# Cross-attention and feed-forward block: opening query sums reordered, gate weights loaded by SyncE

## The chip, the cores and the metric

One core of a Trainium2 chip runs the whole program. The metric is the time of one execution in device microseconds (us); lower is better. Engines are named as in the profile: PE (TensorE matmul) with PEld (its weight loads), DVE (VectorE), ACT (ScalarE), POOL (GpSimd) and SP (SyncE, which here only issues DMAs).

## The reference

The block is one transformer layer on x of 8 sequences, 128 tokens, 512 features, all in float32:

```
x = x + attn(layernorm(x), ctx) @ Wo          # 32 query heads, 8 key heads, head size 128
x = x + ffn(layernorm(x))
attn: q, k with rotary tables; logits = 30 * tanh(q.k * 0.0884 / 30); mask; softmax; times v
ffn:  (silu(x @ dq(w1).T) * (x @ dq(w2).T)) @ dq(w3).T        # 1376 hidden units
dq:   blocks of 64 weights; each weight, over its block's largest magnitude,
      is moved to the nearest of 16 levels and scaled back
```

So there are three parts of work: projections and attention, the rounding of w1, w2 and w3 to 16 levels, and the feed-forward products with the rounded weights.

## The kernel before, in words

**Number format.** Products run as three float32r matmuls (function product, L165): each operand is split into a high part (ScalarE cast, L155) and a low part (subtraction, L156, on VectorE or GpSimd, whichever the caller names). A product over 512 features is 12 matmuls of 128x128 by 512 columns.

**Stages.** First come the key and value projections of all heads and the four query products of the first unit (u = 0), with results in DRAM. Then the attention loop runs over N = 64 steps i (L763). A unit u is a key head kv and half of the batch; a step is one batch entry of one unit, with its four query heads (G = 4). A step issues, for TensorE and in this order: a query product of the next unit (q_proj, tile pq), the output projection of step i-3 (project, tile po), the transposition of step i-2 (turn, tile pt_a), the weighted values of step i-1 (values, tile pv) and the scores of step i (scores, tile pl). All engines run their instructions in program order, so what stands ahead of an instruction on its engine holds it back.

**What follows a query product.** rope (L455) copies the two halves of pq crosswise on ScalarE (L463, L464), multiplies by the cosine on VectorE (L465) and by the sine on GpSimd (L466), and returns the sum (L467), which the caller places. For the first two units the sum is on VectorE, and for u = 1 the cosine product stays in pq's own PSUM bank, so the bank is free only after the sum. pq and pt_a share two banks (tag q); pl, pt_y and others share one (tag s).

**What follows the scores.** Two ScalarE activations (tanh and exp, L682, L683) and the mask on GpSimd (L685); then the values matmuls, a reciprocal and a product on VectorE (tile ad, L694, L695), and the transposition.

**Opening steps.** Step 0 makes query products 0 and 1 of unit 1, step 1 product 2, step 2 product 3, step 3 none. The output projection weights of the first head (load_o, tile wo, named o 0 0 to o 0 3 in the table due) are split in these steps: the first two on VectorE, the last two on GpSimd. Step 0 splits the first at its end. In step 1 the third product's rope comes at the head, its sum behind the values, then the second weight's split. In step 2 the fourth product's rope comes behind the transposition and its sum behind the values.

**Quantization.** A generator (quantize, L376) rounds w1, w2 and w3 unit by unit. Each unit (up to 128x1024 values, tile w) is loaded by SyncE with its scales (tiles s_w), multiplied by the inverse scale on GpSimd (L206), compared with 15 bounds, one ScalarE activation (nm, L196) and one VectorE operation (nc, L202) each, multiplied by the scale on VectorE (L238 or L280) and split (a cast and a GpSimd subtraction, tile w3t or dqt). pump(n) runs the generator for n credits of about one bound each; it is called twice a step. The rounded w1 and w2 go to DRAM (w12t_d) and come back in the feed-forward part; the rounded w3 stays in SBUF. In a unit of w3 the next unit's weights and inverse scales are loaded at bound 6 (L234, L228), the product of L206 is at bound 13, and its own scales are loaded at bound 2.

**Feed-forward.** xn (L150) are the normalized rows, transposed into pt_y and split into xT (normal2, turned). gate_up (L731) makes a gate product (tile pg) and an up product (tile pu) of one of two batch halves and one of 11 blocks of 128 hidden units. load_w12(h) (L726) loads the two 512 KB weights of block h, in a pool of six buffers shared with the query weights. Blocks 0 to 2 are loaded in the last three attention steps, the others in the loop of L868 at n = 1, 2, 5, 7, 9, 11, 13 and 15, after that iteration's pump. The loads are issued by GpSimd. At last the down products (tile pd, L893, L903) use w3t.

Of the kernel before, what the change touches and what calls it, by code (L numbers as in the profile page):

```python
# [11 lines left out]
F32 = mybir.dt.float32  # L12
# [11 lines left out]
G = NH // NKV  # L24
# [38 lines left out]
def block_kernel(ctx: ExitStack, tc: tile.TileContext, x, ctxt, mask, wq, wk, wv, wo, w1, w2, w3, w12t, w3_t,  # L63
                 rope_tab, nf_bias, out):
    nc = tc.nc
# [14 lines left out]
    w12t_d = dram.tile([NHT, 2, P, 2, KT, P], F32, name="w12t_d")  # L80
# [130 lines left out]
    class Down(Unit):  # L211
# [30 lines left out]
        def store(self, h):  # L242
            pool, tag, bufs = (f1, "w3t", 8) if h < 8 else (nf, "nf_t", 2) if h < 10 else (xp, "wide", 2)
            t = w3t[h] = pool.tile([P, 2, KT, P], F32R, tag=tag, name=f"w3t_{h}", bufs=bufs)
            own = t.rearrange("p i k c -> p i (k c)")[:self.p].rearrange("p i (c e) -> p i e c", e=4)
            split(own[:, 0], own[:, 1], self.part(self.w, h).rearrange("p (e c) -> p e c", e=4), Q)
# [44 lines left out]
    class Scales:  # L291
# [23 lines left out]
        def turn(self, tag):  # L315
            pt = bank(tag, f"pt_ar_{self.h}")[:2 * 16, :P]
            E.transpose(pt, self.s.rearrange("p t b -> p (t b)"), ident)

            def later():
                t = nf.tile([2 * 16, P], F32, tag="nf_st", name=f"art_{self.h}", bufs=1)  # L320
                S.copy(t, pt)
                nc.sync.dma_start(scale_d.rearrange("t j b h -> (t j b) h")[:, self.h * P:(self.h + 1) * P], t)
            stored.append(later)

    class Scales3:
# [3 lines left out]
        s = cp.tile([P, 2, nb], F32, name="ar3")  # L329
# [75 lines left out]
    def pump(n):  # L405

        credit[0] += n
        while credit[0] > 0:
            credit[0] -= next(stream, n + credit[0])
# [7 lines left out]
    def end_store():  # L417
        if stored:
            stored.pop()()
# [7 lines left out]
    with ExitStack() as c1:  # L427
# [41 lines left out]
        wqt, todo = {}, {}  # L469

        def load_q(kv, g):
            wqt[kv, g], todo["q", kv, g] = columns(wq, kv * G + g, f"wq_{kv}_{g}")

        def q_proj(u, g):
            kv, half = divmod(u, 2)
            if g == 0:
                qr[u] = a1.tile([P, 4, G, T], F32, tag="qr", name=f"qr_{u}", bufs=2)
            pq = bank("q", f"pq_{u}_{g}")
            w, t = wqt[kv, g], xT[half]
            product(pq, [((w[:, 0, k], w[:, 1, k]), (t[:, 0, k], t[:, 1, k])) for k in range(KT)])  # L480
            return lambda: rope(qr[u][:, :, g, :], pq, cosq, sgnq, f"q{u}_{g}", V if u < 2 else None, u == 1)


        with ExitStack() as c3:
# [134 lines left out]
            xn, turned = {}, {}  # L619
# [38 lines left out]
        def load_o(kv, g):  # L658
            h = kv * G + g
            raw = stage(wo[h * HD:(h + 1) * HD], [P, D], f"wo_{kv}_{g}")  # L660
            t = wot[kv, g] = at.tile([P, 2, D], F32R, tag="wo", name=f"wo_{kv}_{g}", bufs=8)
            todo["o", kv, g] = lambda: split(t[:, 0], t[:, 1], raw, Q if kv or g > 1 else V)

        def load_kv(kv):
            for half in range(2):
                krt[kv, half] = at.tile([P, 512], F32, tag="kr", name=f"krt_{kv}_{half}", bufs=4)
                nc.sync.dma_start(krt[kv, half], kr_d[kv, half])
            vt[kv] = at.tile([P, B, HD + 1], F32, tag="v", name=f"vt_{kv}")
            nc.sync.dma_start(vt[kv][:, :, :HD], v_d[kv])
            Q.memset(vt[kv][:, :, HD:], 1.0)  # L670

        def where(i):
            u, bb = divmod(i, 4)
            return u, u // 2, (u % 2) * 4 + bb, bb
# [12 lines left out]
        def values(i):  # L687
            u, kv, b, bb = where(i)
            ad[i] = at.tile([P, G, HD], F32, tag="ad", name=f"ad_{i}")
            pv = ps.tile([P, G, 256], F32, tag="pv", name=f"pv_{i}", bufs=1)  # L690
            for g in range(G):
                E.matmul(pv[:, g, :HD + 1], em[i][:, g], vt[kv][:, b], start=True, stop=True)  # L692
            rs = tp.tile([P, G], F32, tag="rs", name=f"rs_{i}")
            V.reciprocal(rs.unsqueeze(2), pv[:, :, HD:HD + 1])  # L694
            V.tensor_tensor(ad[i], pv[:, :, :HD], rs.unsqueeze(2).to_broadcast([P, G, HD]), ALU.mult)  # L695
# [5 lines left out]
        def project(i):  # L701
            u, kv, b, bb = where(i)
            po = bank("wo", f"po_{i}")
            product(po, [((aT[i][:, 0, g], aT[i][:, 1, g]), (wot[kv, g][:, 0], wot[kv, g][:, 1]))
                         for g in range(G)])
            V.tensor_tensor(acc[b], acc[b], po, ALU.add)
# [9 lines left out]
        def normal2(b, xn, tag):  # L716
            if b % 4 == 0:
                xT2[b // 4] = wide(f"xT2_{b // 4}")
            t = xT2[b // 4]
            own = slice(b % 4 * T, b % 4 * T + T)  # L720
            return transposed(t[:, 0, :, own], t[:, 1, :, own], xn, f"y{b}", tag)


        w12, hT, ups = {}, {}, []

        def load_w12(h):  # L726
            w12[h] = [wp.tile([P, 2, KT, P], F32R, tag="wq", name=f"w12_{h}_{j}", bufs=6) for j in range(2)]
            for j in range(2):
                nc.gpsimd.dma_start(w12[h][j], w12t_d[h, j])

        def gate_up(half, h, pool=None, between=None):  # L731
            t = xT2[half]
# [20 lines left out]
                V.tensor_tensor(hT[half, h // 4][:, h % 4], sg, pu, ALU.mult)  # L753
            return later

        due = {0: [("o", 0, 0)], 1: [("o", 0, g) for g in range(1, G)]}
        xn = {}

        def turned(ks, tags):
            for f in [normal2(k, xn[k], tag) for k, tag in zip(ks, tags)]:  # L760
                f()

        for i in range(N):  # L763
            u, kv, b, bb = where(i)
            s8 = i % 8
            if kv + 1 < NKV:
                if s8 == 0:
                    load_kv(kv + 1)
                if s8 < 4:
                    load_q(kv + 1, s8)  # L770
                else:
                    load_o(kv + 1, s8 - 4)
                due.setdefault(i + (2 if i < 4 else 1), []).append(("q" if s8 < 4 else "o", kv + 1, s8 % 4))
            tiles = {0: (0, 1), 1: (2,), 2: (3,), 3: ()}.get(i, (bb,)) if u + 1 < 2 * NKV else ()
            later = [q_proj(u + 1, g) for g in tiles]
            if i != 2:
                later = [f() for f in later[:1]] + later[1:]
            if i == 0:
                later.pop(0)()
            if i > 3:  # L780
                store()
                end_store()
            pump(1.5 if 2 < i < 58 else 1 if i == 58 else 0)
            if 0 <= i - 3:
                project(i - 3)
            if i in (59, 61):
                ln = LayerNorm((i - 59, i - 58), f"y{i - 59}")
            if 0 <= i - 2:
                turn(i - 2)
            if i == 2:  # L790
                later = [later[0]()]
            if 59 <= i < 63:
                ln.sums(i - 59)
            if 0 <= i - 1:
                values(i - 1)
            if i in (1, 2):

                later.pop(0)()
                if i == 1:
                    todo[due[1].pop(0)]()  # L800
            scores(i)
            if i == 0:
                later = [later[0]()]
            if i == 61:
                xn.update({k: pair.rows(k, "xn") for k in (0, 1)})
            for f in later:
                f()
            pump(1.65 if 2 < i < 58 else 2 if i == 58 else 0)
            if i == 62:
                turned((0, 1), "qq")  # L810
            if i in (60, 62):
                ln.finish(Q)
                pair = ln
            for k in due.pop(i, ()):
                todo[k]()
            if i >= 61:
                load_w12(i - 61)
# [3 lines left out]
        turned((2,), "s")  # L821
        turn(N - 2)
        values(N - 1)
        turned((3,), "s")
        ln = LayerNorm((4, 5), "y1")
        ln.sums(4)
        ln.sums(5)
# [40 lines left out]
    for n, (half, h) in enumerate(order):  # L868
        evac()
        evac = gate_up(half, h, f1)  # L870
        pump((3.6 if n < last - 3 else 2.6) if n > 0 else 0)
        store()
        if n in w12_at:
            load_w12(w12_at[n])
        if n >= last - 3:
            split_h(*to_split.pop(0))
# [4 lines left out]
    for b, i in down:  # L881
# [5 lines left out]
        for h in range(4 * i, min(NHT, 4 * i + 4)):  # L887
            m = min(P, H - h * P)
            t, s = w3t[h].rearrange("p i k c -> p i (k c)"), hs[b, i]
# [7 lines left out]
        elif i == 2:  # L897
            o = f1.tile([P, D], F32, tag="o", name=f"o_{b}", bufs=4)
# [41 lines left out]
```

## Time and profile before

| | |
|---|---|
| median of 3 runs | 783.3 us (782.45 to 1315.04) |
| profiled execution | 782.62 us, span 780.9 us, granted TensorE clock 1.000 |
| outside the span | 1.7 us |
| gate loads (w, L729) | 22 of 512 KB, 4.7 us median from issue to landing |
| s_w loads of 64 KB | 86, on SyncE |
| all DMA | 102.44 MB, mean 131 GB/s |

A timeline line of the profile has the start (us from the span's start), the duration, engine, line and operation, the tiles written and read, the shape and the number of instructions merged; in brackets stands the idle time ahead of it and what ended that. A line "A <- B: x, n, y" in a list of waits says that A waited for B x us in total, n times, y at most. Matmuls are pipelined, so consecutive ones overlap in the timeline; starts are the better measure.

### The profile page before, as it was taken

The page shows a single profiled execution, that of the slowest core. Times are in us where ns is not written, and L with a number is a line of the kernel's source. Part 1 is how long each engine was busy: PE and PEld are TensorE (multiplying, and loading weights), DVE is VectorE, ACT ScalarE, POOL GpSimd, SP SyncE. Part 2 cuts the span into 40 slices and gives each one's busy share as a digit, 9 for nine tenths or more (in the row PEclk, how much of TensorE's full clock was granted, in tenths as well). Part 3 has the DMA queues.
Part 4 walks back from the last instruction along what each step waited for, and adds up shares of the span by engine and source line. Part 5 has one row for each costly group of instructions (what it writes and reads, how often), then busy time and mean ns, then how long its engine had stood idle before and what let it go on. Part 6 is the DMA issues. An engine that isn't in the chain of part 4 may idle for free.

```text
span 780.9 us, 11199 instructions
## 1 busy us (share of the span) xinstructions
PE 775.2 (99%) x3737; PEld 627.7 (80%) x3737; DVE 626.8 (80%) x839; ACT 585.4 (75%) x821; POOL 468.3 (60%) x412
## 2 busy tenths in 40 slices
PE   9999999999999999999999999999999999999998
PEld 7888877878878787887888888878778888888887
DVE  6768877888887887888888878888778697899971
ACT  7458668888897979798787879898742686789740
POOL 3569537887878778877778787878651222332100
PEclk9999999999999999999999999999999999999999
DMA  7966753546255615536245523413123235633011
GB/s 231 300 206 199 220 160 99 174 124 176 56 173 138 199 45 165 148 93 208 65 146 159 155 71 112 134 60 116 60 103 108 61 97 166 179 118 112 1 54 55
DMA packets 73329, 102.44 MB, mean 131 GB/s; under 512 B 7832, under 2 KB 42840, under 8 KB 73272
## 3 DMA queue, kind: packets, MB, share of 16 engines
q1 hardware_dynamic: 70104, 90.19, 38.6%
q0 software_dynamic: 3168, 11.54, 4.7%
q8 instruction: 30, 0.49, 0.3%
q14 instruction: 27, 0.22, 0.1%
HBM read 79.32 MB, written 22.38 MB: 130 GB/s over the span
## 4 chain that ended last, share of the span: by engine, by line
PE 97%; DVE 1%; POOL 1%; ACT 1%; issue 0%; POOLq 0%
PE pq L172 22%; PE po L172 22%; PE pd L172 8%; PE pg L172 8%; PE pu L172 8%; PE pv L692 7%; PE pl L679 7%; PE pk L172 6%; PE pvp L172 6%; PE pt_a L162 3%; PE warm L91 0%; PE pt_x L162 0%; DVE xn_y L150 0%; PE pt_y L162 0%; DVE xT L156 0%
## 5 line engine op out<-in xcount | busy, mean ns | idle before, releaser
L202 DVE SCALAR_TENSOR_TENSOR nc_w<-nm_w,nc_w 128x1024 f32<-128x1024 bf16 (+1 forms) x238 | 284.6, 1196 | 56.5 <-ACT nm_w L196 45.4
L196 ACT ACTIVATE nm_w<-w_w,bias 128x1024 bf16<-128x1024 f32 (+1 forms) x255 | 275.8, 1115 | 25.8 <-POOL w_w L206 17.1
L172 PE MATMUL pq<-xT,wq 128*128 128x512 f32 x768 | 209.1, 422 | 0.0
L172 PEld LDWEIGHTS pq<-xT,wq 128*128 128x128 f32 x768 | 143.9, 188 | 55.8 <-issue 24.4
L172 PE MATMUL po<-wo,aT 128*128 128x512 f32 x768 | 188.7, 394 | 0.0
L172 PEld LDWEIGHTS po<-wo,aT 128*128 128x128 f32 x768 | 143.3, 188 | 33.3 <-issue 2.4
L685 POOL TENSOR_TENSOR th<-th,mt 128x512 f32<-128x512 f32 x64 | 83.6, 1307 | 86.0 <-ACT th L683 78.1
L466 POOL TENSOR_TENSOR rs_q<-rs_q,sgnq 128x512 f32<-128x512 f32 x64 | 82.5, 1289 | 15.1 <-ACT rs_q L464 15.1
L682 ACT ACTIVATE th<-pl 128x512 f32<-128x512 f32 x64 | 38.3, 598 | 51.0 <-PE pl L679 47.9
L467 POOL TENSOR_TENSOR qr<-rc_q,rs_q 128x512 f32<-128x512 f32 x56 | 72.6, 1297 | 0.0
L692 PE MATMUL pv<-vt,th 128*128 128x129 f32 x512 | 67.9, 276 | 0.1
L679 PE MATMUL pl<-qr,krt 128*128 128x512 f32 x128 | 65.6, 594 | 0.0
L172 PE MATMUL pg<-xT,w 128*128 128x512 f32 x264 | 63.8, 390 | 0.0
L172 PE MATMUL pu<-xT,w 128*128 128x512 f32 x264 | 63.5, 389 | 0.0
L692 PEld LDWEIGHTS pv<-vt,th 128*128 128x128 f32 x512 | 62.2, 192 | 0.7 <-POOL th L685 0.7
L172 PE MATMUL pd<-w3t,hs 128*128 128x512 f32 (+3 forms) x297 | 60.6, 366 | 0.0
L206 POOL TENSOR_TENSOR w_w<-w_w,s_w 128x1024 f32<-128x1024 f32 (+1 forms) x17 | 40.0, 2351 | 32.8 <-DMA s_w<-scale_d 31.2
L172 PEld LDWEIGHTS pd<-w3t,hs 128*128 128x128 f32 (+1 forms) x297 | 51.4, 189 | 9.2
L172 PEld LDWEIGHTS pu<-xT,w 128*128 128x128 f32 x264 | 49.5, 188 | 10.3
L172 PEld LDWEIGHTS pg<-xT,w 128*128 128x128 f32 x264 | 49.3, 188 | 10.1
L156 POOL TENSOR_TENSOR w3t<-w_w,w3t 128x512 fp32r<-128x512 f32 (+1 forms) x11 | 17.2, 1565 | 64.8 <-ACT w3t L155 64.8
L155 ACT CAST aT<-pt_a 128x512 fp32r<-128x512 f32 x64 | 36.5, 571 | 26.0 <-PE pt_a L162 26.0
(119 smaller groups left out, 1105.2 us busy)
## 6 DMA issues: line engine op xcount, KB each, us to landing
w12t_d<-dqt SPq DMA_DIRECT2D x22, 512.0 KB
w<-w12t_d POOLq DMA_DIRECT2D x22, 512.0 KB, 4.7
s_w<-scale_d SPq DMA_DIRECT2D x40, 256.0 KB
raw_wq<-in_L_xattn_Wq SPq DMA_DIRECT2D x32, 256.0 KB
raw_wo<-in_L_xattn_Wo SPq DMA_DIRECT2D x32, 256.0 KB
s_w<-scale_d SPq DMA_DIRECT2D x86, 64.0 KB
ws<-in_L_ffn_w SPq DMA_DIRECT2D x20, 256.0 KB
w_w<-in_w12t SPq DMA_DIRECT2D x10, 512.0 KB
```

The lines of the kernel that those rows point to most:

```text
L155: S.copy(hi, src)
L162: E.transpose(pt[:, k * P:(k + 1) * P], src[:, k * P:(k + 1) * P], ident)
L172: E.matmul(out, a, b, start=start and i + j == 0, stop=stop and i == n - 1 and j == 2)
L196: S.activation(m, self.w, AF.Relu, bias=bias[:self.p, i:i + 1], scale=BIG if up else -BIG)
L202: V.scalar_tensor_tensor(self.c, m, step, self.c, ALU.min, ALU.subtract if i == POS[0] else ALU.add)
L206: Q.tensor_tensor(self.w, self.w, self.s, ALU.mult)
L466: Q.tensor_tensor(s, s, every(sgn), ALU.mult)
L467: return lambda: (engine or Q).tensor_tensor(dst, c, s, ALU.add)
L679: E.matmul(pl, krt[kv, u % 2][:, bb * T:(bb + 1) * T], qr[u][:, bb].rearrange("p g t -> p (g t)"), start=True, stop=True)
L682: S.activation(th, pl, AF.Tanh, scale=ATTN_MULT / CAP)
L685: Q.tensor_tensor(em[i], em[i], mt.unsqueeze(1).to_broadcast([P, G, T]), ALU.mult)
L692: E.matmul(pv[:, g, :HD + 1], em[i][:, g], vt[kv][:, b], start=True, stop=True)
```

## The change

Four edits. The gate loads are issued by SyncE, with the tile viewed as float32. The first projection weight's split moves from the end of step 0 to step 1, directly behind the third query product's rope. The third query sum moves ahead of the values of step 1. The fourth query product's rope and sum move behind the scores of step 2. With these, the two pumps of step 3 run 0.5 and 2.65 credits in place of 1.5 and 1.65, and the last tile turned ahead of the feed-forward part takes a bank of tag q in place of s. The arithmetic is the same.

```diff
         def load_w12(h):
             w12[h] = [wp.tile([P, 2, KT, P], F32R, tag="wq", name=f"w12_{h}_{j}", bufs=6) for j in range(2)]
             for j in range(2):
-                nc.gpsimd.dma_start(w12[h][j], w12t_d[h, j])
+                nc.sync.dma_start(w12[h][j].bitcast(F32), w12t_d[h, j])
...
-        due = {0: [("o", 0, 0)], 1: [("o", 0, g) for g in range(1, G)]}
+        due = {1: [("o", 0, g) for g in range(G)]}
...
             if i == 0:
                 later.pop(0)()
+            if i == 1:
+                todo[due[1].pop(0)]()
             if i > 3:
                 store()
                 end_store()
-            pump(1.5 if 2 < i < 58 else 1 if i == 58 else 0)
+            pump(1.5 if 3 < i < 58 else 1 if i == 58 else 0.5 if i == 3 else 0)
...
-            if i == 2:
-                later = [later[0]()]
             if 59 <= i < 63:
                 ln.sums(i - 59)
+            if i == 1:
+
+                later.pop(0)()
             if 0 <= i - 1:
                 values(i - 1)
-            if i in (1, 2):
-
-                later.pop(0)()
-                if i == 1:
-                    todo[due[1].pop(0)]()
+            if i == 1:
+                todo[due[1].pop(0)]()
             scores(i)
-            if i == 0:
+            if i in (0, 2):
                 later = [later[0]()]
...
-            pump(1.65 if 2 < i < 58 else 2 if i == 58 else 0)
+            pump(1.65 if 3 < i < 58 else 2 if i == 58 else 2.65 if i == 3 else 0)
...
-        turned((3,), "s")
+        turned((3,), "q")
```

## The prediction

> **What bounds the kernel now.** I read the page first, then TensorE's own waits, then the stretches the change edits, engine by engine.
>
> ```profile
> PE 775.2 (99%) x3737; PEld 627.7 (80%) x3737; DVE 626.8 (80%) x839; ACT 585.4 (75%) x821; POOL 468.3 (60%) x412
> PE 97%; DVE 1%; POOL 1%; ACT 1%; issue 0%; POOLq 0%
> ```
>
> TensorE is 99% busy and is 97% of the chain that ended last. Only a hole in its stream, or a new one, can change the time. Its waits over the span, without the warm-up:
>
> ```profile
> PE pt_a L162 <- DVE qr L467: 0.6, 1, 0.6
> PE pt_y L162 <- DVE xT L156: 0.3, 1, 0.3
> ```
>
> Both lie where the change is. But busy time hides part of a hole, since a matmul lasts longer than its turn (0.39 us against 2.76 us for twelve, 0.23 each). So I compare starts, in the timeline of TensorE at the opening of attention, with those of a later step.
>
> ```profile
> 115.75 3.06 PE L172 MATMUL pq<-xT,wq 128*128 128x512 f32 x12
> ...
> 119.77 1.02 PE L679 MATMUL pl<-qr,krt 128*128 128x512 f32 x2
> 120.83 2.98 PE L172 MATMUL pq<-xT,wq 128*128 128x512 f32 x12
> 124.46 0.63 PE L162 MATMUL pt_a<-ident,ad 128*128 128x128 f32 x4 [0.65 <-DVE qr L467]
> ```
>
> Scores to transposition takes 119.77 to 124.46, 4.69 us. The same sequence later (131.21 less 0.46, to 134.37) takes 3.62. So 1.07 us is lost here: 0.2 net ahead of the product at 120.83, which waits for the bank of the second query sum, and 0.87 behind it, for the third. VectorE's timeline says why:
>
> ```profile
> 119.99 0.69 DVE L467 TENSOR_TENSOR qr<-pq,rs_q 128x512 f32<-128x512 f32 x1 [0.70 <-POOL rs_q L466]
> 120.60 1.70 DVE L156 TENSOR_TENSOR wo<-raw_wo,wo 128x512 fp32r<-128x512 f32 x1
> 122.22 0.69 DVE L465 TENSOR_TENSOR pq<-pq,cosq 128x512 f32<-128x512 f32 x1
> ...
> 123.03 0.69 DVE L695 TENSOR_TENSOR ad<-pv,rs 128x512 f32<-128x512 f32 x1
> 123.63 0.68 DVE L467 TENSOR_TENSOR qr<-pq,rs_q 128x512 f32<-128x512 f32 x1
> ```
>
> The first projection weight's split (1.70 us) sits ahead of the third query's product. The end of attention, GpSimd's timeline:
>
> ```profile
> 584.93 1.30 POOL L729 DMA_DIRECT2D w<-w12t_d  x2
> 586.24 1.30 POOL L685 TENSOR_TENSOR th<-th,mt 128x512 f32<-128x512 f32 x1
> ```
>
> The gate loads hold the last mask back 1.0 us (its exp ended at 585.23). TensorE there:
>
> ```profile
> 587.59 1.16 PE L692 MATMUL pv<-vt,th 128*128 128x129 f32 x8
> 589.08 0.66 PE L162 MATMUL pt_y<-ident,xn_y 128*128 128x128 f32 x4 [0.33 <-DVE xT L156]
> ```
>
> In the feed-forward part TensorE has no hole at all. The queue that gets the loads, SyncE's timeline:
>
> ```profile
> 692.86 0.83 SPq L234 DMA_DIRECT2D w_w<-in_w3t  x2
> 693.73 11.64 SPq L228 DMA_DIRECT2D s_w<-scale_d  x16
> ```
>
> GpSimd, and the product that uses gate load 9:
>
> ```profile
> 688.23 1.10 POOL L729 DMA_DIRECT2D w<-w12t_d  x2
> 691.28 1.56 POOL L156 TENSOR_TENSOR w3t<-w_w,w3t 128x512 fp32r<-128x512 f32 x1 [1.95 <-ACT w3t L155]
> 699.30 2.40 POOL L206 TENSOR_TENSOR w_w<-w_w,s_w 128x1024 f32<-128x1024 f32 x1 [6.46 <-DMA s_w<-scale_d]
> ```
>
> ```profile
> 695.30 2.88 PE L172 MATMUL pg<-xT,w 128*128 128x512 f32 x12
> ```
>
> SyncE's w_w load at 692.86 starts when GpSimd's split ends (691.28 + 1.56 = 692.84). Load 9 was issued at 688.23 on the other queue and did not care.
>
> **The change, part by part.** All sums are against the profiled execution: 782.62 us, span 780.9, 1.7 outside it. It is 0.7 below the 783.3 median of the runs shown.
>
> 1. Opening of attention, third query sum. VectorE has the same five pieces after 120.68, in another order: product (0.69), wo split, sum (0.68), reciprocal (0.17), ad (0.69). With no split ahead of it, the third product runs at 120.68 to 121.3. ScalarE's copies for it (0.58 each) move ahead of the wo cast and end at about 120.0, so GpSimd's rs product (1.28) ends at 121.4 and GpSimd then idles until mask 1 (about 122.6). The split costs 1.70 beside GpSimd work (row above), 1.14 in the next wo split at 124.23, and 0.68 is the same instruction with a PSUM source. Beside an idle GpSimd I take 0.8, nearest to 0.68, so sum 122.1, ad 122.9 to 123.7, transposition at about 123.9: gain 0.55. At 1.70 it starts at 124.75, loss 0.3; the cap is 0.8, where TensorE itself gets there.
>
> 2. Fourth query sum behind scores. The transposition of step 3 does not want its bank: a new tile takes the buffer that was handed back first in program order. (The scale loads at 622.60 wait for GpSimd's w_w product, L206, and start ahead of the VectorE product of the unit before, L238, at 625.75; rotation in turn would have waited for that.) Bank of transposition 0 is back in step 2 ahead of the fourth sum, so transposition 1 takes it, and the query product of step 4 takes the other. From scores 2 at T, by rows: tanh T+1.1 to 1.7, exp to 2.33, two copies to 3.55; GpSimd's mask to 3.7, rs product to 5.0, sum to 5.7. The step-4 product started at T+5.39 (125.82 to 131.21); it comes 0.5 late, of which 0.25 is absorbed by the issue gap that stands there anyway. The wq split of key head 1 also queues behind it on GpSimd (1.29 more, T+6.3), and the third matmul, at T+6.0, needs it. Cost 0.4; bounds 0 (the backlog is worked off) and 1.0 (the whole tile waited for). Mask 2 comes first, no loss. The pump of step 3 gives 0.5 and 2.65 in place of 1.5 and 1.65, the same 3.15: ScalarE has one 1.1 us instruction more behind exp 3; tanh 4 slips by at most that, with 3 us to its mask's reader. Nothing.
>
> Opening: -0.55 + 0.4 = -0.15; bounds -0.8 and +1.3.
>
> 3. End of attention. Three pairs of issues (1.29, 1.30, 1.13) leave GpSimd. Mask 63 runs at 585.27 to 586.57, its values at the natural 587.33 (0.43 behind the transposition at 586.90), 0.26 earlier. xn 2 and 3 took 2.80 beside the issues and 1.97 at 574.22 beside a mask alone, so VectorE is some 0.65 earlier too. The last turned tile goes to bank q, no longer waiting for the s tile's split: 587.33 + 0.90 = 588.23 in place of 589.08. The projection behind follows at 588.66, its third matmul wants aT 62's split at 589.1 (done 0.6 earlier than 589.63: just in time). Gain 0.8; bounds 0 (VectorE no earlier and the projection stalls instead) and 1.0.
>
> 4. Gate loads on SyncE. Loads 0 to 4 are early or wait for the same products as before. The scale loads behind load 4 are needed 20 us later (649.89). From load 5 on the place in SyncE's program counts, by the pump's credits: load 5 behind the w_w and s_w loads at 641.40, load 7 behind those at 665.79, load 9 behind those at 692.86; 6, 8 and 10 follow at once. How long a 512 KB load on SyncE takes to land is not shown. Below: 2.3 (last s_w issue 697.0 to GpSimd's start at 699.30, 64 KB). Above: 4.7 (the same load from GpSimd). I take the middle, 3.5.
>  - Load 5: issue 646.75, lands 650.25, wanted 651.78. Nothing, at 4.7 either.
>  - What loads 5 and 7 no longer do is share the DMA engines with the s_w loads ahead. In before, s_w's last issue at 646.3 was followed by GpSimd at 650.38, 4.1 later, against the 2.3 of the quiet case. So w_w's product comes 1.8 earlier, and VectorE, busy from 654.00 to 677.2 without a hole, with it; at the next unit the loads land 4 us earlier, and VectorE begins it about 3.3 earlier than 678.87.
>  - Load 7: w_w loads 1.75 earlier, issue 669.3, lands 672.8, wanted 673.54. Nothing; 1.1 to 2.3 without the catch-up.
>  - Load 9: GpSimd's split ends 692.84 - 3.3 = 689.5, two w_w and eight s_w issues take 4.55 (692.86 to 697.4), issue 694.1, lands 697.6; wanted 695.30. A new hole of 2.3. Bounds: split at 688.5 (ScalarE bound by TensorE alone) and landing 2.3: 0.05; no catch-up, landing 4.7: 6.8.
>
> The row of 692.86 shows an issuer that stands still until a split is done; SyncE's waits for w3t come to 42.3 us in four, the longest 14.4. [...]
>
> Sum: 782.62 - 0.15 - 0.8 + 2.3 = 784.0 us. Gains of 0.95 are eaten by one new wait.
>
> **The rivals.**
> - A, no catch-up: VectorE or ScalarE set the quantization's pace, the w_w load stays at 692.86, and load 9 is the new bound: 692.86 + 4.55 + 3.5 = 700.9, hole 5.6; with 1.1 for load 7, 788.4; with the upper landing, 791. For it: VectorE is busy 20.5 of 22 us in 684 to 706. Against it: GpSimd waited 8.4 us for s_w in these units, the wait that shrinks. It decides the sign once load 9 issues later than 692.8 (hole over 0.95).
> - B, loads in time: the stream catches up wholly and lands fast, hole 0 to 0.5: 781.7 to 782.2, faster by 0.5 to 0.9. For it: ScalarE's earliest case above. Against: the two w_w and eight s_w issues still stand between.
> - C, the opening turns worse: split 1.70, whole tile waited for: +1.3 instead of -0.15, 785.4.
> - D, more than 2% (15.7 us) either way. TensorE's holes are under 3 us in all, so no such gain; such a loss needs several load waits of the full 6.8.
>
> **How the numbers follow.** Forecast (hole 0.5 to 4, 782.2 to 785.7): 0.50. A 0.25, B 0.16, C 0.06, D 0.03. About 2% is what a measurement of this kernel can tell from no change; forecast, A, B and C all lie within it: same 0.97, slower 0.02, faster 0.01. Range 781.0 to 788.5: the low end is B with the bounds of parts 1 to 3 half used, the high end A with the middle landing. The likeliest case alone has 782.2 to 785.7.
>
> **What would show it.** Opening: the transposition behind the fourth query product starts 0.5 earlier, and the first query product of step 4 has a wait of about 0.5 on the fourth sum. End: last mask right behind its exp, no wait on xT for the last pt_y. Feed-forward: TensorE with one wait on a DMA, at the sixteenth or so gate product, of about 2 us; SyncE with w12 loads behind s_w; GpSimd's waits for s_w shorter than 26.6 us. Wrong if gate products never wait (B), or wait twice or over 5 us (A), or if the opening's transposition still starts 4.69 behind its scores.

## The result, and the profile after

The changed kernel takes 786.3 us in the median of six executions (784.37 to 787.9), the kernel before 783.09 in the same comparison. The ratio, in which the one execution of 1315.04 us is left out as slow, is 1.0036, 95% interval 1.0023 to 1.0048: a loss of a third of a per cent, far inside 2%. Ratios below are also to the kernel before, measured again beside each version; they are not the quotients of the medians, and the brackets are 95% intervals. The profiled execution took 786.38 us with a span of 784.6, 3.7 more than before (780.9).

Starts of the same instructions in the two traces say where the 3.7 us are:

| stretch, by starts on TensorE | before | after | difference |
|---|---|---|---|
| start of the span to scores 0 (pl at 115.03, 115.71) | 115.03 | 115.71 | +0.68 |
| scores 0 to projection of step 4 (po at 134.37, 134.26) | 19.34 | 18.55 | -0.79 |
| to scores 63 (pl at 582.85, 582.81) | 448.48 | 448.55 | +0.07 |
| to the first gate product (pg at 592.70, 591.78) | 9.85 | 8.97 | -0.88 |
| to the gate product of block 9 (pg at 695.30, 697.26) | 102.60 | 105.48 | +2.88 |
| that product's twelve matmuls | 2.72 | 4.42 | +1.70 |
| to the end of the span | 82.88 | 82.92 | +0.04 |

The opening of attention in the changed kernel, TensorE's timeline:

```profile
120.45 1.02 PE L679 MATMUL pl<-qr,krt 128*128 128x512 f32 x2
121.50 2.97 PE L172 MATMUL pq<-xT,wq 128*128 128x512 f32 x12
124.31 0.60 PE L162 MATMUL pt_a<-ident,ad 128*128 128x128 f32 x4
```

Scores to transposition is 3.86 us, 4.69 before. The wait on the third query sum is gone, and the 0.6 us at the start of the product (it waits for the second sum's bank) is still there. VectorE's timeline beside it:

```profile
121.27 0.69 DVE L465 TENSOR_TENSOR pq<-pq,cosq 128x512 f32<-128x512 f32 x1
121.87 0.73 DVE L156 TENSOR_TENSOR wo<-raw_wo,wo 128x512 fp32r<-128x512 f32 x1
```

The split in the second line, which took 1.70 us before, takes 0.73. Beside it GpSimd's products end at 122.05, and its next work, a mask, starts at 123.09.

The query product of step 4, first in TensorE's timeline before, then after, where it starts only behind the fourth sum (done at 131.29 on VectorE). The scores ahead of it start at 130.75 and 130.57, the projection behind it at 134.37 and 134.26.

```profile
131.21 3.33 PE L172 MATMUL pq<-xT,wq 128*128 128x512 f32 x12
```

```profile
131.44 2.98 PE L172 MATMUL pq<-xT,wq 128*128 128x512 f32 x12
```

The end of attention, first GpSimd, then VectorE's two normalized rows, then TensorE:

```profile
585.27 1.41 POOL L685 TENSOR_TENSOR th<-th,mt 128x512 f32<-128x512 f32 x1 [0.33 <-ACT th L683]
```

```profile
584.98 1.98 DVE L150 TENSOR_SCALAR xn_y<-acc,mv_y,y_y 128x512 f32<-128x512 f32 x2 [0.74 <-POOL y_y L110]
```

```profile
587.30 1.06 PE L692 MATMUL pv<-vt,th 128*128 128x129 f32 x8
588.19 0.60 PE L162 MATMUL pt_y<-ident,xn_y 128*128 128x128 f32 x4
```

The last mask starts right behind its exp, and the last turned tile no longer waits. The largest wait of TensorE in the changed kernel (total us, count, longest):

```profile
PE pg L172 <- DMA w<-w12t_d: 2.7, 1, 2.7
```

It is new: one gate product waits for its weights. TensorE's timeline there, and SyncE's:

```profile
691.67 2.88 PE L172 MATMUL pu<-xT,w 128*128 128x512 f32 x12
697.26 4.58 PE L172 MATMUL pg<-xT,w 128*128 128x512 f32 x12 [2.71 <-DMA w<-w12t_d]
701.68 2.91 PE L172 MATMUL pu<-xT,w 128*128 128x512 f32 x12
```

```profile
688.83 0.83 SPq L234 DMA_DIRECT2D w_w<-in_w3t  x2
689.71 3.67 SPq L228 DMA_DIRECT2D s_w<-scale_d  x8
693.48 1.79 SPq L729 DMA_DIRECT2D w<-w12t_d  x4
```

Load 9 stands behind the w_w and s_w loads of a w3 unit, which begin at 688.83 when a GpSimd split ends (687.23 + 1.57 = 688.80). It goes out at 693.48 together with load 10; the product, whose turn was 694.39, starts at 697.26, 3.78 us after the issue. And the product itself lasts longer: starts 697.26 to 701.68 are 4.42 us in place of 2.72. The windows view shows a lower clock there (window, length, busy time with number of instructions of PE, PEld, DVE, ACT and POOL, the granted TensorE clock, the DMA share and GB/s):

```profile
698.00:699.00 1.00, 1.00 (x4) 0.77 (x3) 0.69 (x2) 0.00 (x0) 0.00 (x0) 0.56 1.01 414
699.00:700.00 1.00, 1.00 (x4) 0.81 (x3) 0.00 (x0) 0.00 (x0) 0.00 (x0) 0.50 1.05 430
...
701.00:702.00 1.00, 1.00 (x5) 0.82 (x4) 0.00 (x0) 0.12 (x1) 0.00 (x0) 0.74 0.93 221
```

By the means of these windows the clock is 1.00 up to about 698.1 and 0.50 from there to about 701.5, close behind the hole. The same stretch also has heavy DMA traffic, so the trace alone does not say which of the two slows TensorE.

### The profile page after: what moved, and what is told of

The parts are those of the page before. It is cut to its first block, busy times and chain, and to the rows that moved or that the text cites. A ratio compares the mean times of both kernels' runs of the same rounds, so it can differ in the third digit from the quotient of the medians.

```text
span 784.6 us, 11180 instructions
## 1 busy us (share of the span) xinstructions
PE 776.5 (99%) x3737; PEld 628.1 (80%) x3737; DVE 625.5 (80%) x839; ACT 586.0 (75%) x821; POOL 455.7 (58%) x390
## 4 chain that ended last, share of the span: by engine, by line
PE 92%; DMA 2%; DVE 2%; ACT 2%; SPq 1%; issue 1%; POOL 0%; DVEq 0%; ACTq 0%
PE pq L172 23%; PE po L172 22%; PE pd L172 8%; PE pv L692 7%; PE pl L679 7%; PE pg L172 7%; PE pu L172 6%; PE pvp L172 5%; PE pt_a L162 4%; PE pk L172 3%; DMA kr_d<-kr 1%; DMA raw_c<-in_ctx 1%; ACT nm_w L196 1%; DVE kr L467 1%; DMA w<-w12t_d 0%
## 5 line engine op out<-in xcount | busy, mean ns | idle before, releaser
L172 PE MATMUL pg<-xT,w 128*128 128x512 f32 x264 | 65.4, 398 | 2.7 <-DMA w<-w12t_d 2.7
```

What stands on the lines that cost most here:

```text
L172: E.matmul(out, a, b, start=start and i + j == 0, stop=stop and i == n - 1 and j == 2)
```

## The experiments

The theory after the result: the edits of attention gain 1.67 us, load 9 behind w_w costs a hole of 2.88, and the hole lowers the clock, another 1.70. Rivals: the traffic slows the matmuls; SyncE's loads cost something in general; the gain at the end of attention comes from the bank alone; the fourth sum's move costs something.

**Filling the hole.** 24 transpositions of the identity, into a bank that is not in use, give TensorE work while it waits. They are extra work, and nothing reads them.

```diff
+        if n == 16:
+            idle = bank("s", "idle")
+            for k in range(24):
+                E.transpose(idle[:, k % 4 * P:(k % 4 + 1) * P], ident, ident)
         evac = gate_up(half, h, f1)
```

> The changed kernel with 24 transpositions of the identity (into an unused bank) put ahead of the gate product that waits for load 9; each takes a 0.11 us turn, 2.6 us in all, inside the 2.87 us hole. Theory (the hole itself costs 2.87, and the idle time lowers the granted clock, which costs another 1.70 in the twelve matmuls behind it): the hole stays, the twelve take 2.72 again, granted clock 1.00 there, span 784.6 - 1.7 = 782.9. Rival (the twelve matmuls are slow because loads 9 and 10 move 358 GB/s beside them): unchanged, 4.4 us for the twelve, span 784.6.

Measured 784.58 us, ratio to before 1.0014 (1.0005 to 1.0023), span 782.6. TensorE's timeline:

```profile
694.21 2.78 PE L873 MATMUL idle<-ident 128*128 128x128 f32 x24
696.87 3.01 PE L172 MATMUL pg<-xT,w 128*128 128x512 f32 x12
```

The window from 697 to 702, first in the changed kernel, then here:

```profile
697.00:702.00 5.00, 4.74 (x14) 3.77 (x15) 1.69 (x2) 0.12 (x1) 0.45 (x1) 0.66 1.00 358
```

```profile
697.00:702.00 5.00, 5.00 (x23) 4.09 (x24) 1.50 (x2) 2.09 (x3) 0.40 (x1) 1.00 0.94 349
```

The product still comes late (696.87 against a turn at 694.21), with nearly the same traffic beside it (349 GB/s, 358 in the changed kernel), and its twelve matmuls take 2.85 us (the next product starts at 699.72) at clock 1.00: 1.57 less than in the changed kernel, if 0.13 more than the 2.72 expected. So the traffic is not the reason; of the two, TensorE's idle time of 2.71 us is left.

**Half filled.** The same with 12 transpositions.

> The changed kernel with 12 identity transpositions at the head of the wait for load 9 instead of 24: TensorE works 1.3 of the 2.87 us and idles about 1.5. It asks how long a hole lowers the granted clock. If the drop comes with any hole that can be seen, the clock falls as in the changed kernel (0.5 to 0.8 behind it, twelve matmuls in 3.5 to 4.4 us, span about 784.0). If it takes a hole nearer to 2.87, the clock stays at 1.00 and the span is that of the full fill, about 782.6.

Measured 784.82 us, ratio 1.002 (1.001 to 1.0029), span 782.2, clock 1.00 throughout. TensorE:

```profile
693.59 1.47 PE L873 MATMUL idle<-ident 128*128 128x128 f32 x12
696.46 3.00 PE L172 MATMUL pg<-xT,w 128*128 128x512 f32 x12 [1.40 <-DMA w<-w12t_d]
```

A hole of 1.40 us left the clock alone, one of 2.71 was followed by half the clock. None of the 21 executions of the two filled versions has a mean clock below 0.999; four of the six of the changed kernel do. One of those six has a mean clock of 1.000 and a span of 782.6, 1.8 under the next, so the long hole seems not to do it every time; that execution was not traced. Where between 1.40 and 2.71 the line is, and what decides, stays open.

**Load 9 one iteration earlier.** It then stands ahead of the w_w loads in SyncE's program; its buffer is free by then.

```diff
-    w12_at = {1: 3, 2: 4, 5: 5, 7: 6, 9: 7, 11: 8, 13: 9, 15: 10}
+    w12_at = {1: 3, 2: 4, 5: 5, 7: 6, 9: 7, 11: 8, 12: 9, 15: 10}
```

> The changed kernel with load 9 issued one iteration earlier (n = 12 in place of 13), so that it stands ahead of the w_w and s_w loads in SyncE's program; all else as changed. Theory (load 9 behind w_w is the whole loss): no wait at the tenth block's gate product, span 784.6 - 2.87 - 1.70 = 780.0, median about 781.8, faster than before by 0.9 to 1.7. Rival (SyncE issue costs by itself, by sharing with the s_w loads or by a wait that moves to another block): span 782 or more, with a wait at another gate product or at a down product.

Measured 781.32 us, ratio 0.9972 (0.9961 to 0.9983), span 780.0. SyncE's timeline:

```profile
675.14 0.84 SPq L729 DMA_DIRECT2D w<-w12t_d  x2
688.82 0.81 SPq L234 DMA_DIRECT2D w_w<-in_w3t  x2
```

Load 9 goes out at 675.14, 18 us before its old place, and no gate product waits. One number in one line takes back the whole loss of the feed-forward part (4.6 us of span) and makes the change faster than the kernel before. Its ratio is the lowest of the versions tried, though the intervals of the next ones overlap with it.

**All loads from 5 on one iteration earlier** (n = 4, 6, 8, 10, 12, 14):

> The changed kernel with each load from 5 on issued so that it stands ahead of the w_w and s_w loads of its iteration (n = 4, 6, 8, 10, 12, 14 in place of 5, 7, 9, 11, 13, 15). Theory: as with load 9 alone, span 780.0, no wait. A rival: the s_w loads now share the DMA engines with the gate loads again, as in the kernel before, ScalarE falls back by 2 to 4 us per unit and the last w3t split comes as late as before (749 us); TensorE wants it about 751, so at most 1 us is lost at the down products: 780.0 to 781.0.

Measured 781.87 us, ratio 0.9978 (0.9969 to 0.9986), span 779.7. The other loads were not late and gain nothing; the intervals of the two versions overlap.

**Loads 3 to 10 back on GpSimd,** 0 to 2 on SyncE:

```diff
-                nc.sync.dma_start(w12[h][j].bitcast(F32), w12t_d[h, j])
+                if h < 3:
+                    nc.sync.dma_start(w12[h][j].bitcast(F32), w12t_d[h, j])
+                else:
+                    nc.gpsimd.dma_start(w12[h][j], w12t_d[h, j])
```

> The changed kernel with loads 0 to 2 on SyncE and loads 3 to 10 on GpSimd as before. Theory: the end of attention keeps its 0.87 us, the feed-forward part is as before, span 784.6 - 4.57 = 780.0. Rival (the gain at the end of attention comes from the tile's bank alone, or GpSimd's issue in the feed-forward part costs something): 780.0 still for the first, over 780.5 for the second.

Measured 781.95 us, ratio 0.9978 (0.9969 to 0.9987), span 779.6. Scores 63 to the first gate product is 8.95 us (582.38 to 591.33), 8.97 in the changed kernel: the whole gain of SyncE as issuer is in the first three loads. This run also shows what a gate load beside the s_w loads costs them, which the prediction put down to shared DMA engines. GpSimd's w_w product here, with load 7 beside the s_w loads (beside load 5 it starts at 648.94):

```profile
673.43 2.40 POOL L206 TENSOR_TENSOR w_w<-w_w,s_w 128x1024 f32<-128x1024 f32 x1 [8.07 <-DMA s_w<-scale_d]
```

and in the changed kernel, with load 7 queued behind (with load 5 behind, 647.05):

```profile
668.76 2.39 POOL L206 TENSOR_TENSOR w_w<-w_w,s_w 128x1024 f32<-128x1024 f32 x1 [6.31 <-DMA s_w<-scale_d]
```

The two products come 1.9 and 4.7 us earlier there, with the first gate product 0.45 later. From SyncE's issue of the w_w loads to the product it is 8.90 and 9.08 us here (issues at 640.04 and 664.35), 6.56 and 6.28 there (640.49 and 662.48). In the kernel before, where load 5 moves together with the s_w loads, the DMA share is 1.02 to 1.17 in each window of 1 us from 644 to 649. Queueing behind the scales does speed the quantization up, as the prediction had it. On TensorE nothing waits for that speed in this version; in the changed kernel load 9 does, since it goes out only after a split of that quantization.

**The opening's edits alone** (loads on GpSimd, last turned tile in bank s):

> The kernel before with only the opening steps' edits (first weight's split, third and fourth query sum, pumps of step 3). Theory (the opening's gain stands by itself): from scores 0 to the output projection of step 4 it takes 18.55 us as in the changed kernel, against 19.34 before; from scores 63 to the first gate product 9.85 as before; span shorter by 0.8. Rival (the opening's gain is given back later in attention, because ScalarE starts step 4 with one instruction more): the product and projection starts around 575 us come as early relative to scores 0 as before, no gain.

Measured 783.16 us against 782.95, ratio 0.9994 (0.9985 to 1.0004), span 779.9. Scores 0 to the projection of step 4 (114.80 to 133.43) is 18.63 us, 0.71 less than before, and from scores 0 to scores 63 (581.97) it is 467.17 us against 467.82: 0.65 of the lead is still there. The trace shows the gain and where it lies; by the times alone it cannot be told from nothing.

**The opening and the bank,** all loads on GpSimd:

> The changed kernel with all gate loads on GpSimd: opening edits and the last turned tile in bank q. Theory (the end's 0.88 us comes mostly from taking the issues off GpSimd): the bank alone gives 0.2 to 0.3, since VectorE still finishes the normalized rows at the same time; scores 63 to first gate product 9.6 us. Rival (it is the bank): 9.0.

Measured 782.25 us, ratio 0.9987 (0.9978 to 0.9996), span 780.4. Scores 63 (582.71) to the first gate product (592.30) is 9.59 us: the bank alone gives 0.26 of the 0.88. VectorE's timeline shows what keeps the rest:

```profile
584.89 2.80 DVE L150 TENSOR_SCALAR xn_y<-acc,mv_y,y_y 128x512 f32<-128x512 f32 x2 [0.75 <-POOL y_y L110]
```

With GpSimd's issues and its mask beside them the two normalized rows take 2.80 us, as before; in the changed kernel, beside the mask alone, 1.98.

**Load 9 early, the last turned tile in bank s again:**

> The changed kernel with load 9 one iteration earlier and the last turned tile back in bank s. Theory (the bank is worth 0.3 once the issues are gone): scores 63 to first gate product 9.3 us, with a wait of the last pt_y on xT; span 0.3 over that of load 9 early. Rival (the bank is worth nothing, the issues on GpSimd are all): 9.0.

Measured 782.37 us, ratio 0.9984 (0.9974 to 0.9994), span 779.6. Scores 63 (582.14) to the first gate product (591.35) is 9.21 us, 0.24 over the changed kernel's 8.97. The last pt_y starts 1.13 behind its values in place of 0.89. So the bank is worth about 0.25 with or without the issues, and the issues the other 0.63. The span went the other way by 0.4; scores 0 starts 0.66 earlier in this trace (114.94 against 115.60), where the two programs are still the same.

**Load 9 early, the fourth query sum back in its old place:**

```diff
+            if i == 2:
+                later = [later[0]()]
...
             if 0 <= i - 1:
                 values(i - 1)
+            if i == 2:
+                later.pop(0)()
...
-            if i in (0, 2):
+            if i == 0:
                 later = [later[0]()]
```

> The changed kernel with load 9 one iteration earlier and the fourth query product's rope and sum where they were before (behind the transposition and behind the values of step 2). From scores 2 to the output projection of step 4 the kernel before took 8.55 us, the changed one 8.62. Theory (moving the fourth sum costs 0.07 here, as the traces have it, not the 0.4 of the prediction): 8.55. A rival (the move helps: mask 2 on GpSimd now waits for the sine product ahead of it, 1.3 us, and the values with it): 8.7 or more.

Measured 782.12 us, ratio 0.9987 (0.9978 to 0.9996), span 780.0. Scores 2 (125.46) to the projection of step 4 (134.25) is 8.79 us; with the sum behind the scores it is 8.62. TensorE:

```profile
129.09 0.60 PE L162 MATMUL pt_a<-ident,ad 128*128 128x128 f32 x4
129.66 1.16 PE L692 MATMUL pv<-vt,th 128*128 128x129 f32 x8
```

GpSimd:

```profile
128.30 1.30 POOL L685 TENSOR_TENSOR th<-th,mt 128x512 f32<-128x512 f32 x1
```

The values start 0.57 behind the transposition in place of 0.43, and last 0.1 longer: mask 2 is late on GpSimd, behind the sine product that began at 127.05 (its exp ended at 127.84). My theory (8.55) was wrong and the rival right: once the opening has been tightened, the move helps, by 0.17 us. In the kernel before, mask 2 was not late (128.27, with its exp done at 128.20).

## Why the prediction was right, and where its sizes were off

It said 784.0, little change, a gain of about 1 eaten by one new wait on load 9. That is what happened, at the place it named: one gate product waits, load 9 stands behind w_w and s_w, and the last mask follows its exp. GpSimd's waits for s_w in the feed-forward part fell from 26.6 to 23.7 us. The size was not right. The profiled 786.38 is 2.4 over the sum and lies outside the likeliest case (782.2 to 785.7); the range of 781.0 to 788.5 holds it only because rival A reached that far. The terms:

- **Part 1 and 2, the opening** (-0.15 predicted, -0.79 measured). Half of the 0.64 is the third sum: its mechanism went as worked out (the split took 0.73, 0.8 taken), but the transposition no longer waits at all, and scores 0 to scores 2 gained 0.86 (10.79 to 9.93) where 0.55 had been taken. The other half is the cost of 0.4 for the fourth sum, which was wrong. The product of step 4 did start late (131.44, 0.87 behind its scores in place of 0.46), but its twelve matmuls then took 2.82 in place of 3.16, so only 0.07 was left. The wq split held the third matmul's weights back by 0.15 us, and the issue gap of 0.24 that stood there before is gone. What the move buys in the tightened opening, mask 2 free of the sine product, was not priced; it is worth the 0.17 of the last experiment.
- **Part 3, the end** (-0.8 predicted, -0.88 measured). Right, in its cause too: 0.63 by the issues, 0.25 by the bank.
- **Part 4, the hole** (2.3 predicted, 2.88 measured). The catch-up was there, a little smaller than worked out: the w_w loads went out at 688.83, which is 689.74 on the axis of the kernel before (its products come 0.91 later), 3.1 us earlier where 3.3 had been taken. So load 9 went out 0.3 later than predicted (693.48, or 694.39 on that axis, against 694.1). The landing was 0.3 short as well: 3.78 us from issue to the product's start, where 3.5 had been taken between 2.3 and 4.7.
- **Left out: the clock** (+1.70). A hole was priced at its length. In the profiled execution 2.71 us of idle were followed by 3.4 us at half the clock. Rival A's hole of 5.6 had no such term either, and what a hole of that length costs in clock no run shows; for the forecast's 2.3 the runs leave it open, between 1.40 without a drop and 2.71 with one.
- **Left out: the first 115 us** (+0.68), in which the two programs are the same. Scores 0 starts at 115.03 in the profile before, 115.71 after, and at 115.46, 115.60, 115.43, 115.17, 114.80, 115.61, 114.94, 115.50 and 114.71 in the nine experiments. The eleven profiles range from 114.71 to 115.71 with no order by version, which I take for chance of the single execution; the changed kernel's profile is the latest of them. Most of its 0.68 is one wait early in the program, on VectorE, which only one of the other ten traces has (the fourth sum in its old place, 0.66):

```profile
37.35 0.28 PE L317 MATMUL pt_ar<-ident,ar 128*32 128x128 f32 x1 [0.56 <-DVE mt L558]
```

In the kernel before, the same transposition starts at 36.71 without a wait. Why VectorE is late there stays open.

The errors of the opening (0.64 too little gain) and of the hole (0.58 too short) cancel, and that is luck; what is left of the 2.4 is the clock and the first 115 us.

Rival A (no catch-up, hole 5.6) did not come, though its time of 788.4 lies nearer to the measured 786.4 than the forecast's 784.0; B failed because the w_w and s_w issues do stand between; C did not come, since the opening gained. The sum had no term for the change of issuer by itself in the feed-forward part, only for load 9's place in the queue. The runs with loads 3 to 10 on GpSimd and with load 9 early agree with that (188.27 and 188.20 us from the first gate product to the end of the span, 188.20 before); the place of one load in its queue was worth 4.6 us of span. At the end of attention the change of issuer was worth more than the issuer's own time: VectorE's two normalized rows were 0.82 us shorter too. The prediction also took about 2% as what a measurement can tell from no change; the interval here tells 0.36% from none.

## What to carry to other kernels

When a DMA moves to another engine's queue, list what stands ahead of it there in program order and what each of those waits for; here the second half of the loads stood behind such waits, one of them came too late, and moving it one iteration up turned a loss of 0.36% into a gain of 0.28%. A hole in TensorE's stream can cost more than its length: 2.71 us of idle were followed by 1.70 us more at the lower clock, 1.40 us were not. To judge fractions of a microsecond, compare starts between two fixed instructions in each trace, since spans differ by up to 1.0 us before the first changed instruction.

## What the runs showed of the hardware

- A hole of 2.71 us in TensorE's work was followed by 3.4 us at granted clock 0.50, starting about 0.9 us after work resumed; a hole of 1.40 us was not, nor was the long hole filled with transpositions.
- VectorE's split with two SBUF inputs took 1.70 us beside GpSimd products and 0.73 with GpSimd idle for all but its first 0.2 us; the two normalized rows took 2.80 us beside two DMA issues of GpSimd and a mask, 1.98 beside a mask alone.
- A 512 KB load from SyncE reached its reader 3.8 us after the issue, with two loads of 256 KB and eight of 64 KB just ahead of it.
- What stood ahead on an engine held back what followed: on GpSimd the last mask, whose exp had ended at 585.23, started at 586.24 behind two gate-load issues, and at 585.27 with the loads on SyncE; on SyncE load 9 went out at 693.48, behind w_w and s_w loads that began at 688.83, when a split had ended at 688.80.
